# Tap combinations of the first image's convolution on Pool and ACT instead of DVE, and two column combinations per step instead of three

## The chip, the core and the metric

The kernel runs on one core of one Trainium2 chip. The core has a matrix engine (PE, with a separate weight load that the profile calls PEld), three engines for elementwise work (DVE, ACT and Pool, also called GpSimd), and a queue engine (SP) that here only issues DMAs. Each engine works through its own list of instructions in order, and waits on semaphores for the others. The metric is the device time of one execution in microseconds (us).

## The reference, cut to what matters

Eight images of 32 x 32 positions and 256 channels pass through a layer of convolution beside attention with relative positions, then a dense attention layer and a feed-forward layer. Only the first layer matters here:

```
# per image, after a group norm over 32 groups of channels
conv_out = conv3x3(x, conv_w) + conv_b            # 256 -> 192 channels, SAME
k, q, v  = split(x @ qkv_w + qkv_b)               # 64 channels each, 8 heads of 8
logits   = q . k + rel_w(q, key_rel_w) + rel_h(q, key_rel_h)   # 1024 x 1024 a head
attn     = softmax(logits) @ v @ attn_w + attn_b  # 64 channels
x        = x + concat(conv_out, attn)
```

All data and weights are float32.

## The kernel before, in words

**Convolution.** The 3x3 convolution is computed four output columns at a time with combinations of the input columns and of the taps (a Winograd scheme along a row). Along a row, the taps w0, w1 and w2 of `conv_w` become six combinations, and the columns of the normed image become six differences; then six sets of products are made on PE and summed. The tap combinations are made once, by `conv_weights` (lines 298 to 321), into the tile `convw`; each of the six has 128 partitions x 1152 elements. They are

```
cw0 = -(w0 + w1 + w2)/6      cw3 = (w0 - 2 w1 + 4 w2)/24
cw1 = -(w0 - w1 + w2)/6      cw4 = w0/4
cw2 = (w0 + 2 w1 + 4 w2)/24  cw5 = w2
```

Before, DVE makes the six two-input sums (L306, L308, L311, L314, L316, L319), and ACT the two that only scale or copy (L304, L305) and the four scalings in place (L309, L312, L317, L320). The raw taps lie in the tile `taps`.

The column differences are made for every image by `by_fours` (L370 to L411) into the tile `gdif`, on DVE. It reads the normed image x and yields after each small group of operations, so that a caller can spread it over other work. The products are in `conv_steps` (matmuls at L560, tile pc, copied by ACT at L569).

**The norm.** `norm_steps` (L329 to L367) transposes the image on PE, takes statistics on DVE, averages them over groups by two small matmuls (gm, then pv) and forms 1/sqrt in `one_over_root` (L90 to L102): rv = pv + eps on DVE (L96), a logarithm and an exponential on ACT (ry L97, gr L98), then on DVE a correction of four tiny operations (L99 to L102, of which L99 and L100 multiply rv by gr). With gr, DVE writes the normed image x (L360). Pool adds the biases l0b to the image T there (L340).

**Keys, queries and relative logits.** `input_steps` (L418 to L527) makes keys and queries (pk on PE L423; kq by ACT L433 and DVE L440), values (pvv L444), and sends kq by 16 DMAs on SP's queue into the tiles km (L458). The fixed patterns of km come from `key_patterns`: DVE makes a small table oh (L281 to L283), Pool copies and adds it (L289, L290). Then come the relative logits: 256 small matmuls along the width and 256 along the height, in four groups (prel, L495). Each group's two halves are copied out by DVE (L507) and ACT (L509), into rw for the width and into rh for the height. rw is stored to memory (rwd, L512) and also transposed on PE into rwq (tpw L520, copies L522 and L524). The difference table reld for the height is made in turns by DVE and Pool (L262, L265).

**Attention.** A `Unit` is half of one group of heads. Its tile F is gathered by DMAs on SP from rh (L590), kq (L594) and rwd (L601); then follow scores on PE (lg, L618), their maxima on DVE (L626), scores the other way (st, L658), exponentials on ACT (L666) and products with the values (L675). Steps of the convolution are mixed in between.

**Buffers.** The tiles F, x, rw and taps share one pool of three buffers (tag "F"). A new tile of that tag waits for the last reader of the tile whose buffer it takes.

**Order.** For the first image all of this is a prologue (L1024 to L1044), in a block where the order of PE's and DVE's instructions is the one written, and ACT, Pool and SP are ordered by the scheduler. After the norm, the key patterns and the first 12 steps of `input_steps`, a loop runs over the remaining steps, and after each step it takes three steps of `other`, which is the chain of `by_fours` and `conv_weights`. What is left of `other` follows the loop.

Of the kernel before, what the change touches and what calls it, by code (L numbers as in the profile page):

```python
# [3 lines left out]

# [9 lines left out]
ALU = mybir.AluOpType  # L14
# [22 lines left out]
def kernel(  # L37
# [26 lines left out]
    nc = tc.nc  # L64
# [39 lines left out]
    with ExitStack() as ph:  # L104
# [70 lines left out]
        taps = work.tile([P, 4096], FP, tag="F", name="taps", bufs=3)[:, 0 : 9 * KC * CO]  # L175
# [98 lines left out]
        def key_patterns():  # L274

            KM = []
            oh = wp.tile([P, 16 + DH], FP, tag="oh", name="oh")  # L280
            nc.vector.tensor_copy(oh[:, 0:1], esel[:, 0:1])  # L281
            nc.vector.tensor_tensor(oh[:, 1:16], esel[:, 1:16], esel[:, 0:1].to_broadcast([P, 15]), ALU.add)
            nc.vector.tensor_copy(oh[:, 16:24], esel[:, 24:32])  # L283
            for i in range(NG):
                km = wp.tile([P, 2, 4, P], FP, tag=f"km{i}", name=f"km{i}")
                for a in range(2):
                    kv = km[:, a].rearrange("p g (y x) -> p g y x", y=8)
                    for g in range(4):
                        nc.gpsimd.tensor_copy(kv[:, g], oh[:, 0:16].unsqueeze(1).to_broadcast([P, 8, 16]))  # L289
                        nc.gpsimd.tensor_tensor(  # L290
                            kv[:, g], kv[:, g], oh[:, 16:24].unsqueeze(2).to_broadcast([P, 8, 16]), ALU.add
                        )
                KM.append(km)
            return KM
# [3 lines left out]
        def conv_weights(taps):  # L298


            taps = taps.rearrange("p (a b n) -> p b a n", a=3, b=3)
            w0, w1, w2 = (taps[:, i] for i in range(3))
            cw = [convw[:, v] for v in range(NV)]
            nc.scalar.mul(cw[4], w0, 0.25)  # L304
            nc.scalar.copy(cw[5], w2)  # L305
            nc.vector.tensor_tensor(cw[1], w0, w2, ALU.add)  # L306
            yield
            nc.vector.tensor_tensor(cw[0], cw[1], w1, ALU.add)  # L308
            nc.scalar.mul(cw[0], cw[0], -1.0 / 6)  # L309
            yield  # L310
            nc.vector.tensor_tensor(cw[1], cw[1], w1, ALU.subtract)  # L311
            nc.scalar.mul(cw[1], cw[1], -1.0 / 6)  # L312
            yield
            nc.vector.scalar_tensor_tensor(cw[3], w2, 4.0, w0, ALU.mult, ALU.add)  # L314
            yield
            nc.vector.scalar_tensor_tensor(cw[2], w1, 2.0, cw[3], ALU.mult, ALU.add)  # L316
            nc.scalar.mul(cw[2], cw[2], 1.0 / 24)  # L317
            yield
            nc.vector.scalar_tensor_tensor(cw[3], w1, -2.0, cw[3], ALU.mult, ALU.add)  # L319
            nc.scalar.mul(cw[3], cw[3], 1.0 / 24)  # L320
            yield


        def norm_steps(b, held):
# [45 lines left out]
        def by_fours(xn):  # L370


            two = nc.vector.tensor_tensor

            def stt(out, one, factor, two):
                for a in range(2):
                    nc.vector.scalar_tensor_tensor(out[:, a], one[:, a], factor, two[:, a], ALU.mult, ALU.add)

            for part in range(2):
                for kc in range(KC):  # L380
                    d1, d2, d3, d4 = (xn[:, kc, :, :, j].rearrange("p a c x -> p a x c") for j in range(4))
                    v = [gdif[:, i, kc, 1 : HH + 1, :].rearrange("p (a x) c -> p a x c", a=2) for i in range(NV)]
                    if part == 0:

                        stt(v[2], d2, -4.0, d4)
                        yield
                        stt(v[3], d1, -4.0, d3)
                        yield
                        two(v[4], d4, d2, ALU.subtract)
                        two(v[5], d3, d1, ALU.subtract)  # L390
                        yield
                        two(v[0], v[2], v[3], ALU.add)
                        two(v[1], v[2], v[3], ALU.subtract)
                        yield
                        continue

                    stt(v[2], v[5], 2.0, v[4])
                    yield
                    stt(v[3], v[5], -2.0, v[4])
                    yield  # L400


                    stt(v[4], d2, -4.0, v[4])
                    yield
                    stt(v[4][:, :, :, 1:NQ], d4[:, :, :, 0 : NQ - 1], 4.0, v[4][:, :, :, 1:NQ])
                    yield
                    nc.vector.tensor_scalar(v[5], v[5], -4.0, None, ALU.mult)
                    two(v[5], v[5], d3, ALU.subtract)
                    two(v[5][:, :, :, 0 : NQ - 1], v[5][:, :, :, 0 : NQ - 1], d1[:, :, :, 1:NQ], ALU.add)
                    yield  # L410
# [618 lines left out]
        with tc.manual_schedule(engines={mybir.EngineType.PE, mybir.EngineType.DVE}):  # L1029
            held = {}  # L1030
            half_w, half_h, reld_steps = tables()
            for _ in norm_steps(0, held):
                pass
            KM = key_patterns()
            steps = input_steps(0, held)
            for _ in range(4 + NT):
                next(steps)
            reld_steps()
            other = chain(by_fours(held["xn"]), conv_weights(taps))
            for _ in steps:  # L1040
                for _ in range(3):
                    next(other, None)
            for _ in other:
                pass  # L1044
        with tc.manual_schedule(engines={mybir.EngineType.PE, mybir.EngineType.Pool}):
            conv = Conv(0)
            means = []
            for b in range(B):
# [11 lines left out]
                now, held = held, {}  # L1060
# [322 lines left out]
```

## Time and profile before

| what | value |
|---|---|
| median of 3 runs | 2334.63 us (2334.57 to 2335.14) |
| the profiled execution | 2339.52 us, of which its span is 2337.5 us |
| PE busy | 2259.4 us, 97% of the span, mean clock 0.982 |
| DVE busy | 1481.7 us, 63% |
| ACT busy | 955.1 us, 41% |
| Pool busy | 505.3 us, 22% |
| PE busy in the first of 40 slices (58 us each) | 5 tenths |

The profile is of one execution and lists each group of equal instructions as start, duration, engine, line of the code, operation, output and inputs, shapes and count; in brackets stands the idle time of the engine before it and what ended it. In grouped rows the first number after the bar is the busy time and the second the mean duration in ns. PEclk is the clock granted to PE as a share of full speed.

The first 75 us hold all of the prologue. The windows of 5 us in which it ends, with busy time (and count) of PE, PEld, DVE, ACT and Pool, the clock, the share of DMA time and GB/s:

```profile
core 0: us, PE busy (x) PEld busy (x) DVE busy (x) ACT busy (x) POOL busy (x), PEclk, DMA share, GB/s
45.00:50.00 5.00, 4.88 (x128) 4.59 (x124) 4.89 (x14) 0.59 (x1) 0.00 (x0) 0.50 0.37 146
50.00:55.00 5.00, 3.20 (x13) 2.55 (x12) 4.93 (x6) 2.98 (x3) 0.00 (x0) 0.50 0.39 96
55.00:60.00 5.00, 5.00 (x24) 4.61 (x23) 4.88 (x4) 2.35 (x4) 0.00 (x0) 0.80 0.60 112
...
70.00:75.00 5.00, 5.00 (x31) 3.06 (x32) 3.49 (x5) 0.48 (x1) 0.54 (x1) 0.94 0.64 125
```

Between 45 and 60 us DVE is busy nearly throughout, Pool does nothing, and PE works at half of its clock for most of the time.

### The profile page before, as it was taken

The numbers are of one execution on the slowest core, as the hardware profiler recorded it, in microseconds if no ns is written. First come the engines' busy times: TensorE is split into PE (matmuls) and PEld (weight loads), VectorE is DVE, ScalarE is ACT, GpSimd is POOL, SyncE is SP. The second block draws the span as 40 slices with busy tenths as digits, with TensorE's granted clock in tenths as the row PEclk, the third lists the DMA queues.
The fourth block names the chain that finished last, engine by engine and source line by source line (L and its number), as shares of the span: only waits on it lengthen the run. The fifth ranks groups of instructions, "written<-read, shape, count | busy, mean of one in ns | idle before, by whom it ended". The sixth has DMA issues, their size and how long they took to land. (4 is left out here: it accounts for less than half of the span.)

```text
span 2337.5 us, 41910 instructions
## 1 busy us (share of the span) xinstructions
PE 2259.4 (97%) x17273; PEld 1284.4 (55%) x17273; DVE 1481.7 (63%) x2717; ACT 955.1 (41%) x1645; POOL 505.3 (22%) x478
## 2 busy tenths in 40 slices
PE   5999999999999999999999999999998699999998
PEld 5535753664367437733763475357533566666665
DVE  7777587658756775777477748765872624444443
ACT  2255336434643563256325532553364223333332
POOL 3301240213031203300340034012301022222220
PEclk7999999999999999999999999999998799999999
DMA  3520352125122502250333025202420312222200
GB/s 105 103 50 10 58 104 39 41 48 102 22 56 42 109 5 60 56 93 3 60 89 61 7 56 105 45 27 47 82 38 1 108 50 78 78 74 78 72 37 27
DMA packets 71471, 135.85 MB, mean 58 GB/s; under 512 B 12001, under 2 KB 24169, under 8 KB 69233
## 3 DMA queue, kind: packets, MB, share of 16 engines
q1 hardware_dynamic: 65488, 115.47, 23.5%
q0 software_dynamic: 3056, 15.73, 2.0%
q8 instruction: 137, 2.24, 0.4%
q10 hardware_dynamic: 2736, 1.97, 0.3%
q14 instruction: 54, 0.43, 0.1%
HBM read 53.43 MB, written 25.17 MB: 34 GB/s over the span
## 5 line engine op out<-in xcount | busy, mean ns | idle before, releaser
L626 DVE TENSOR_REDUCE my<-lg 128x32 f32<-128x1024 f32 x512 | 617.4, 1222 | 166.3 <-PE st L658 124.9
L666 ACT ACTIVATE PT<-st 128x512 f32<-128x512 f32 (+1 forms) x944 | 542.2, 632 | 313.6 <-PE st L658 309.9
L658 PE MATMUL st<-F,km 32*128 32x512 f32 x2048 | 536.9, 640 | 8.2 <-DMA F<-mb 8.2
L618 PE MATMUL lg<-km,F 24*128 24x512 f32 x2048 | 504.9, 637 | 1.7 <-DMA F<-rh 1.7
L675 PE MATMUL po<-PT,vall 128*32 128x256 f32 (+1 forms) x3200 | 312.5, 452 | 2.4 <-ACT PT L666 2.4
L675 PEld LDWEIGHTS po<-PT,vall 128*32 128x32 f32 x3200 | 66.0, 108 | 312.8 <-issue 279.5
L618 PEld LDWEIGHTS lg<-km,F 24*128 24x128 f32 x2048 | 144.1, 183 | 163.7 <-issue 122.7
L560 PE MATMUL pc<-convw,gdif 128*128 128x192 f32 x1152 | 229.4, 342 | 0.7 <-ACT convw L309 0.7
L1296 PE MATMUL phd<-n2T,w 128*128 128x512 f32 x512 | 223.7, 595 | 0.0
L1313 PE MATMUL py<-w,hT 128*128 128x256 f32 x1024 | 223.6, 379 | 0.0
L658 PEld LDWEIGHTS st<-F,km 32*128 32x128 f32 x2048 | 175.6, 183 | 78.2 <-issue 40.5
L560 PEld LDWEIGHTS pc<-convw,gdif 128*128 128x128 f32 x1152 | 186.9, 192 | 56.4 <-issue 32.0
L1313 PEld LDWEIGHTS py<-w,hT 128*128 128x128 f32 x1024 | 194.6, 190 | 33.3 <-issue 7.7
L340 POOL TENSOR_TENSOR T<-T,l0b 128x2048 f32<-128x2048 f32 x8 | 36.3, 4534 | 617.6 <-PE tpx L333 617.6
L1320 DVE TENSOR_TENSOR r<-py,n 128x256 f32<-128x256 f32 x64 | 27.2, 425 | 213.0 <-PE py L1313 213.0
L1296 PEld LDWEIGHTS phd<-n2T,w 128*128 128x128 f32 x512 | 97.2, 191 | 116.1 <-issue 108.9
L846 POOL TENSOR_TENSOR T<-T,n 128x256 f32<-128x256 f32 x64 | 47.4, 749 | 392.4 <-DVE n L832 392.4
L1303 ACT ACTIVATE hT<-phd,b1c 128x512 f32<-128x512 f32 x128 | 86.3, 686 | 98.3 <-PE phd L1296 98.1
L569 ACT COPY m<-pc 128x384 f32<-128x384 f32 x48 | 23.0, 480 | 242.6 <-PE pc L560 198.1
L901 PE MATMUL lg<-qkv 128*128 128x512 f32 x256 | 121.1, 595 | 0.0
L910 DVE TENSOR_REDUCE nm<-lg 128x1 f32<-128x1024 f32 x64 | 78.1, 1221 | 67.5 <-PE lg L901 67.5
L932 PE MATMUL po<-pt,qkv 128*128 128x256 f32 x512 | 116.5, 380 | 0.0
(250 smaller groups left out, 2584.7 us busy)
## 6 DMA issues: line engine op xcount, KB each, us to landing
F<-rh SPq DMA_DIRECT2D x256, 128.0 KB
F<-kq SPq DMA_DIRECT2D x256, 64.0 KB
F<-rwd SPq DMA_DIRECT2D x256, 64.0 KB
w<-in_L_ffn_W_dram SPq DMA_DIRECT2D x32, 512.0 KB
rwd<-rw SPq DMA_DIRECT2D x16, 512.0 KB
Td<-T POOLq DMA_DIRECT2D x8, 1024.0 KB, 4.2
T<-Td SPq DMA_DIRECT2D x8, 1024.0 KB
out_dram<-yo SPq DMA_DIRECT2D x16, 512.0 KB
```

The source lines that it names most:

```text
L560: nc.tensor.matmul(pc[:, v, :], lhsT=gflat[:, 2 * pair + v, kc, at : at + P], rhs=convw[:, 2 * pair + v, dy, kc * CO : (kc + 1) * CO], sta ...
L618: nc.tensor.matmul(lg[:, a, :], lhsT=self.F[r : r + 24, a, 0, i * P : (i + 1) * P], rhs=KM[self.g][r : r + 24, a].rearrange("p e k -> p (e ...
L626: nc.vector.tensor_reduce(my[:, :, hl], lg.rearrange("p a (y x) -> p y a x", y=WW), AX.XY, ALU.max)
L658: nc.tensor.matmul(st[:, i, :] if len(heads) > 1 else st, lhsT=KM[self.g][r : r + 32, a, e, :], rhs=self.F[r : r + 32, a, e, :], start=Tru ...
L666: nc.scalar.activation(self.pts[j][:, hs, :], st, AF.Exp)
L675: nc.tensor.matmul(self.po[32 * hl : 32 * hl + 32, cols], lhsT=vall[:, j, h * (DH + 1) : h * (DH + 1) + 32], rhs=self.pts[j][:, hl, cols], ...
L901: nc.tensor.matmul(lg[:, h, :], lhsT=qk[0][:, i * P : (i + 1) * P], rhs=qk[1][:, h * 512 : (h + 1) * 512], start=True, stop=True,)
L910: nc.vector.tensor_reduce(nm, lg, AX.X, ALU.max, negate=True)
L932: nc.tensor.matmul(po[:, 0:IB], lhsT=v1[:, jc, :], rhs=pt[:, jc, :], start=jc == 0, stop=jc == NT - 1)
L1296: nc.tensor.matmul(phd, lhsT=ws[k][0][:, kc, f * P : (f + 1) * P], rhs=n2T[:, kc, q * 512 : (q + 1) * 512], start=kc == 0, stop=kc == KC - 1,)
L1303: nc.scalar.activation(hT[:, k * NF + f, :], phd, AF.Gelu, bias=b1c[:, f, k * B + b : k * B + b + 1])
L1313: nc.tensor.matmul(py, lhsT=hT[:, k * NF + f, j * P : (j + 1) * P], rhs=ws[k][1][:, f, :], start=k == 0 and f == 0, stop=k == TOPK - 1 and ...
```

## The change

`conv_weights` is no longer a generator that runs behind `by_fours`. It is called once, before the loop over the steps. Its six sums go to Pool, as plain two-input additions and subtractions; what DVE had fused into them (4 w2 and 2 w1) is made by two more scalings on ACT, in the places of cw3 and cw4, so that cw4 is written with its own value last. The loop takes two steps of `other` after each step, which is now `by_fours` alone. Nothing else differs; the images after the first use the same code as before.

```
+            add = nc.gpsimd.tensor_tensor
+            nc.scalar.copy(cw[5], w2)
+
+            nc.scalar.mul(cw[3], w2, 4.0)
+            nc.scalar.mul(cw[4], w1, 2.0)
+            add(cw[1], w0, w2, ALU.add)
+            add(cw[0], cw[1], w1, ALU.add)
+            nc.scalar.mul(cw[0], cw[0], -1.0 / 6)
+            add(cw[1], cw[1], w1, ALU.subtract)
+            nc.scalar.mul(cw[1], cw[1], -1.0 / 6)
+            add(cw[3], cw[3], w0, ALU.add)
+            add(cw[2], cw[3], cw[4], ALU.add)
+            nc.scalar.mul(cw[2], cw[2], 1.0 / 24)
+            add(cw[3], cw[3], cw[4], ALU.subtract)
+            nc.scalar.mul(cw[3], cw[3], 1.0 / 24)
             nc.scalar.mul(cw[4], w0, 0.25)
-            nc.scalar.copy(cw[5], w2)
-            nc.vector.tensor_tensor(cw[1], w0, w2, ALU.add)
-            yield
-            nc.vector.tensor_tensor(cw[0], cw[1], w1, ALU.add)
-            nc.scalar.mul(cw[0], cw[0], -1.0 / 6)
-            yield
-            nc.vector.tensor_tensor(cw[1], cw[1], w1, ALU.subtract)
-            nc.scalar.mul(cw[1], cw[1], -1.0 / 6)
-            yield
-            nc.vector.scalar_tensor_tensor(cw[3], w2, 4.0, w0, ALU.mult, ALU.add)
-            yield
-            nc.vector.scalar_tensor_tensor(cw[2], w1, 2.0, cw[3], ALU.mult, ALU.add)
-            nc.scalar.mul(cw[2], cw[2], 1.0 / 24)
-            yield
-            nc.vector.scalar_tensor_tensor(cw[3], w1, -2.0, cw[3], ALU.mult, ALU.add)
-            nc.scalar.mul(cw[3], cw[3], 1.0 / 24)
-            yield
...
             reld_steps()
-            other = chain(by_fours(held["xn"]), conv_weights(taps))
+            conv_weights(taps)
+            other = by_fours(held["xn"])
             for _ in steps:
-                for _ in range(3):
+                for _ in range(2):
                     next(other, None)
             for _ in other:
                 pass
```

Pool's and ACT's orders are the scheduler's in both kernels. In the program that is built from the changed kernel, Pool's six sums stand behind its last two reld operations and ahead of the km patterns, in the order cw1 = w0 + w2, cw3 = 4 w2 + w0, cw0, cw2, cw1, cw3. On ACT the order is: the copy to cw5, the scalings to 4 w2 and 2 w1, the scaling of cw0, ry (the logarithm of the norm), the scaling of cw2, gr (its exponential), the scalings of cw1 and cw3, cw4, and then the two kq operations.

## The prediction

> **What bounds the kernel now.** I read the page's busy shares first: TensorE (PE) is busy for 2259.4 of 2337.5 us, 97%. Its clock row then names the weak places, and the first slice is the worst (5 tenths busy). Everything the change touches runs once, in the prologue of the first image, so I left the page and read the timeline of the first 75 us engine by engine. From about 71 us on PE has no gaps, so what counts is one number: how much earlier or later PE reaches that unbroken work. The timelines of ACT, DVE and Pool before the first matmuls of the image show (start, duration, engine, line, tiles):
>
> ```profile
> 19.56 0.20 ACT L97 ACTIVATE ry<-rv 128x2 f32<-128x2 f32 x1 [1.97 <-DVE rv L96]
> 19.79 0.20 ACT L98 ACTIVATE gr<-ry 128x2 f32<-128x2 f32 x1
> ...
> 17.48 0.46 DVE L348 TENSOR_TENSOR dm<-gmv,gm 128x2 f32<-128x2 f32 x1
> 17.98 0.51 DVE L349 TENSOR_TENSOR dm<-dm 128x2 f32<-128x2 f32 x1
> 18.53 0.16 DVE L350 TENSOR_TENSOR dm<-dm,gmv 128x2 f32<-128x2 f32 x1
> ...
> 20.82 0.74 DVE L360 TENSOR_SCALAR x<-xT,gm,gr 128x512 f32<-128x512 f32 x1
> ...
> 17.32 1.15 POOL L265 TENSOR_TENSOR reld<-bdh 128x192 f32<-128x192 f32 x2
> ```
>
> All of the image waits for one thin chain: rv on DVE, Ln and Exp (ry, gr) on ACT, two tiny products and a correction on DVE, then x at 20.82. PE's pk follows at 21.61. ACT is idle for 1.97 us before ry, so today nothing stands in that chain's way.
>
> The other end is the start of attention (SP's and PE's timelines):
>
> ```profile
> 50.17 0.68 SPq L590 DMA_DIRECT2D F<-rh  x1
> ...
> 59.55 1.12 PE L618 MATMUL lg<-km,F 24*128 24x512 f32 x2
> 62.38 3.29 PE L618 MATMUL lg<-km,F 24*128 24x512 f32 x6 [1.72 <-DMA F<-rh]
> 65.61 4.21 PE L560 MATMUL pc<-convw,gdif 128*128 128x192 f32 x12
> 69.74 1.54 PE L618 MATMUL lg<-km,F 24*128 24x512 f32 x8
> 71.22 2.06 PE L560 MATMUL pc<-convw,gdif 128*128 128x192 f32 x11
> ```
>
> The first scores wait 1.72 us for a DMA into F. That series began at 50.17, because F took the buffer of x, which DVE reads until 50.11 (last column combination).
>
> **What leaves DVE.** Six operations of 128x1152, at 50.03 to 58.81, 1.35 or 1.36 us each: 8.1 us. PE's first conv (54.02) waited for the ACT scaling of one of them. With them early, conv matmuls fill the gaps around the tpw transposes.
>
> **What Pool gets.** Six adds of 128x1152. Pool shows no such shape; these groups are near (busy us, mean ns):
>
> ```profile
> L1287 POOL TENSOR_TENSOR T<-T,bet 128x1024 f32<-128x1024 f32 x16 | 40.3, 2516 | 0.0
> L340 POOL TENSOR_TENSOR T<-T,l0b 128x2048 f32<-128x2048 f32 x8 | 36.3, 4534 | 617.6 <-PE tpx L333 617.6
> ```
>
> Scaled by width: 4534 x 1152/2048 = 2.55 us, 2516 x 1152/1024 = 2.83. The second row includes waits behind DVE, so I take 2.6. Pool is free at 18.47, when its two reld operations end. The built order puts the adds there in the order cw1, cw3, cw0, cw2, cw1, cw3, ahead of the km patterns. They end at 21.1, 23.7, 26.3, 28.9, 31.5 and 34.1. The km patterns (23.73 now) need oh, which DVE makes after x, so they move with x and pay nothing of their own. SP's km DMAs need them and kq and move alike.
>
> **What ACT gets, and what is queued behind it.** ACT's order is made by the scheduler: copy and two scalings, then the cw0 scaling (waits for the third add), **ry**, the cw2 scaling (waits for the fourth add), **gr**, then the rest. So the thin chain stands behind two waits. cw0 ends at 26.3 + 1.16 = 27.5 and ry runs; cw2 ends at 28.9 + 1.16 = 30.1; gr runs to 30.3 instead of 19.99. Loss so far: 10.3 us. The two scalings and cw4 that follow end near 36.5, before kq needs ACT: nothing. The delay that the first add gives dm (18.53) is hidden, since ry can't run before 27.5.
>
> **The two products behind gr.** Now DVE forms rv x gr twice, both inputs in SBUF, while Pool is in its fifth and sixth add. The row first: DVE's L348 and L349 took 0.46 and 0.51 us while Pool's two reld ran, and L350, just after them, 0.16. So each such operation loses about 0.3 us to a Pool operation of 0.6. The Trainium skill, "SBUF — State Buffer", section "SBUF: two separate sides", says more: the port pair is an exclusive lock for a whole instruction, and a DVE operation with two SBUF inputs blocks fully against a Pool operation that reads SBUF. By the row as a fixed 0.3 us, x comes 0.6 later still: shift 10.9. By the rule the first product waits for the fifth add's end (31.5), the second for the sixth's (34.1): 34.1 + 0.05 + 0.44 (today's 20.38 to 20.82) puts x at 34.6, a shift of 13.7. In the later images L348 ended right when L340's 4.53 us on Pool ended (1.00 us at 194.46, Pool until 195.44), which speaks for the rule. I take **13.7**; 10.3 is the other end.
>
> **What comes back.** All in a frame shifted by 13.7, so that old times can be compared. DVE now does two column steps between copies of relative logits: rw is copied 1.0 us earlier (37.48 to 36.5: the 1.0 us of L389 and L390) the first time and 2.1 earlier the second (42.20 to 40.1), and the first rh copy ends at 44.15. The first F now takes the buffer of taps, free since the adds, so its DMAs wait only for that rh copy: 44.18 instead of 50.17. **6.0 us** back. The second unit's F now waits for the last column combination instead, but its DMAs stood at 67.4 and aren't needed for another 20 us: nothing. The score waiting at 62.38 starts at 56.4.
>
> The rest hangs on the clock. The windows of 5 us (columns: busy and count of PE, weight loads, DVE, ACT, Pool; clock; DMA share; GB/s):
>
> ```profile
> 60.00:65.00 5.00, 3.28 (x8) 0.95 (x6) 1.23 (x1) 1.20 (x2) 3.08 (x4) 0.88 0.59 126
> 65.00:70.00 5.00, 5.00 (x17) 3.96 (x20) 1.23 (x1) 0.00 (x0) 0.00 (x0) 0.50 0.60 81
> ```
>
> After a window with little PE work the clock was 0.50 for 65 to 70 us, and twelve conv matmuls took 4.21 us there against about 2.2 later. If the new gap doesn't cause that, six scores (paced by maxima of 1.23) take 1.8, twelve conv 2.1 (2.06 x 12/11 x 0.94, the clock of 70 to 75), eight scores 1.54: 56.4 + 5.4 = 61.8, where 71.22 stood. Back: **9.4 us**. If it does, the old durations stay and only 6.0 come back.
>
> The Trainium skill, "TensorE: Matmul & The Clock Gate", section "Part 1: The HAM clock gate", lets the clock fall after an idle window of about 3.4 us. The gap here was 1.72 us and the clock fell all the same, in a window that held mostly scores, which use 24 of 128 rows. By the rule taken literally the clock never falls here and 9.4 come back; by the row a similar stall of 1.7 us can do it again and 6.0 come back. I lean to 9.4, because the conv matmuls that moved forward stand next to the gap and fill its window with full-array work.
>
> **Sum.** +13.7 - 9.4 = **+4.3 us**. Against the profiled execution: 2339.52 to 2343.8. That execution lies 4.9 us above the median of the runs; the difference carries over: 2334.63 + 4.3 = **2338.9 us**, 0.18% slower. About 0.2% (4.7 us) is what a measurement of this kernel can tell from no change, so this sits just inside it.
>
> **Rivals.**
> - *The clock falls again* at the score stall: 13.7 - 6.0 = +7.7, 2342.3. For it: the row above. Against: the conv work beside the gap. It decides as soon as one window of 3.4 us there is mostly scores and waiting.
> - *Pool doesn't block the products* (or its adds are shorter): 10.3 - 9.4 = +0.9, 2335.5; with adds of 2.4 us the fourth ends 0.8 earlier, and the result is even. For it: image 1's rows show only 0.3 us. Against: the later images.
> - *The gain outweighs the wait* (not slower): gr would have to come before the cw2 scaling at run time, which a queue in order excludes; or the stage after 71 us gains from a better clock phase. The regain has to exceed 13.7, so 4.3 us more than I see. With one window of half clock saved later (3.4 us at half speed is 1.7) on top of the unblocked products: 0.9 - 1.7 = -0.8, 2333.8.
> - *F doesn't come earlier*, because its DMAs stay bound by km's DMAs or their own transfers: +13.7, 2348.3. Against: km's end at 39.1, five us before.
>
> **Chances.** Forecast 0.42, clock falls 0.33, unblocked 0.13, F late 0.07, gain 0.05. The forecast's own range is 2336.5 to 2341 (adds of 2.5 to 2.8 move the shift by 0.6 to 1.2, later clock phases by 1.7), a good third of it above the bound. Range 2335.2 to 2343.5: it reaches over the fallen clock and most of the unblocked case. Slower: 0.15 of the forecast, nearly all of the fallen clock and of F late, and the long tail of both: 0.52. Same: 0.44. Faster: 0.04.
>
> **What would show it.** In the profile after: Pool's adds of 2.6 us from 18.5; ry near 27.5, gr near 30; two products of over 1 us each; x near 34.6; F's first DMA near 57.9; the conv that stood at 71.22 near 75.5 with the clock at 1.00 from 70 to 75. If gr stands at 20, or x before 31, the prediction is wrong in its first half; if that conv stands at 79, in its second.

## The result, and the profile after

| | before | changed |
|---|---|---|
| median (range, runs) | 2335.14 us (2334.57 to 2337.86, 5) | 2347.03 us (2345.43 to 2347.64, 5) |
| ratio, 95% interval | | 1.0045 (1.0034 to 1.0056) |
| profiled execution | 2339.52 us | 2345.43 us |
| its span | 2337.5 us | 2343.7 us |

The change made the kernel slower by 0.45%, some 10.5 us of 2335 (the two medians lie 11.9 us apart). The forecast was +4.3 us and 2338.9 us, and its range ended at 2343.5, so the result lies outside it. Note that the two profiled executions differ by only 5.9 us: the one of the kernel before lay 4.9 us above the median that the forecast used, the one of the changed kernel is the fastest of these five. That turns out to be most of the story.

The first half of the prediction stands in the timelines of the changed kernel (start, duration, engine, line, tiles). ACT first, then Pool, then DVE:

```profile
26.36 1.16 ACT L310 ACTIVATE convw<-convw 128x1152 f32<-128x1152 f32 x1 [7.62 <-POOL convw L309]
27.43 0.19 ACT L96 ACTIVATE ry<-rv 128x2 f32<-128x2 f32 x1
28.93 1.16 ACT L315 ACTIVATE convw<-convw 128x1152 f32<-128x1152 f32 x1 [1.32 <-POOL convw L314]
30.00 0.19 ACT L97 ACTIVATE gr<-ry 128x2 f32<-128x2 f32 x1
...
28.86 2.62 POOL L311 TENSOR_TENSOR convw<-convw,taps 128x1152 f32<-128x1152 f32 x1
31.43 2.62 POOL L316 TENSOR_TENSOR convw<-convw 128x1152 f32<-128x1152 f32 x1
...
30.22 1.27 DVE L98 TENSOR_TENSOR rv<-rv,gr 128x2 f32<-128x2 f32 x1 [8.17 <-ACT gr L97]
31.53 2.54 DVE L99 TENSOR_TENSOR rv<-rv,gr 128x2 f32<-128x2 f32 x1
34.10 0.17 DVE L100 TENSOR_SCALAR rv<-rv 128x2 f32<-128x2 f32 x1
34.30 0.16 DVE L101 TENSOR_TENSOR gr<-gr,rv 128x2 f32<-128x2 f32 x1
34.50 2.72 DVE L357 TENSOR_SCALAR x<-xT,gm,gr 128x512 f32<-128x512 f32 x4
```

ry and gr stand behind two scalings that wait for Pool. The two products, 0.16 us of work each, end at 31.49 and 34.07, right where Pool's fifth and sixth add end (31.48 and 34.05). x is at 34.50 instead of 20.82.

The second half, SP's and PE's timelines of the same execution:

```profile
57.98 0.68 SPq L587 DMA_DIRECT2D F<-rh  x1
...
68.84 2.22 PE L615 MATMUL lg<-km,F 24*128 24x512 f32 x6
71.50 1.09 PE L615 MATMUL lg<-km,F 24*128 24x512 f32 x2 [0.43 <-DMA F<-kq]
72.52 3.69 PE L557 MATMUL pc<-convw,gdif 128*128 128x192 f32 x12
76.13 1.30 PE L615 MATMUL lg<-km,F 24*128 24x512 f32 x8
77.36 2.22 PE L557 MATMUL pc<-convw,gdif 128*128 128x192 f32 x12
```

F's first DMA came at 57.98, that is 44.28 in the shifted frame, against 50.17. The block of twelve conv matmuls that stood at 71.22 now stands at 77.36; it is called the second block below. From there on the shift stays near that: 6.14 us here, 6.2 at the end of the span.

### The profile page after: what moved, and what is told of

Same layout as the page of the kernel before. It is cut to its first block, busy times and chain, and to the rows that moved or that the text cites. A ratio compares the mean times of both kernels' runs of the same rounds, so it can differ in the third digit from the quotient of the medians.

```text
span 2343.7 us, 41912 instructions
## 1 busy us (share of the span) xinstructions
PE 2256.7 (96%) x17273; PEld 1283.4 (55%) x17273; DVE 1482.1 (63%) x2711; ACT 957.3 (41%) x1647; POOL 520.6 (22%) x484
## 5 line engine op out<-in xcount | busy, mean ns | idle before, releaser
L1301 ACT ACTIVATE hT<-phd,b1c 128x512 f32<-128x512 f32 x128 | 86.3, 686 | 98.5 <-PE phd L1294 98.3
```

Source lines behind the costliest of these rows:

```text
L1301: nc.scalar.activation(hT[:, k * NF + f, :], phd, AF.Gelu, bias=b1c[:, f, k * B + b : k * B + b + 1])
```

## The experiments

**The kernel before, once more.** Its timed runs lay up to 5 us under its profiled one, so here is another profiled execution of the unchanged kernel.

> The kernel before, once more, to see what differs between its profiled execution (2339.52 us) and its timed runs (2334.6 to 2337.9). Theory (clock beside the first scores): in an execution near 2335 us the clock does not fall to half at about 64 us, the twelve conv matmuls that took 4.21 us at 65.61 take about 2.2, and the conv that stood at 71.22 us stands near 67.5. Rival (the 4.9 us lie elsewhere, in the half-clock stretches at 1753 to 1873 us): the first 80 us look as in the first profile and the late stretches are shorter.

The profiled execution took 2334.93 us. 13 runs lay between 2334.93 and 2340.29, median 2336.94. PE's timeline at the same place:

```profile
60.62 1.12 PE L618 MATMUL lg<-km,F 24*128 24x512 f32 x2
62.21 2.45 PE L618 MATMUL lg<-km,F 24*128 24x512 f32 x6 [0.47 <-DMA F<-rh]
64.59 2.22 PE L560 MATMUL pc<-convw,gdif 128*128 128x192 f32 x12
66.73 1.14 PE L618 MATMUL lg<-km,F 24*128 24x512 f32 x8
67.81 2.22 PE L560 MATMUL pc<-convw,gdif 128*128 128x192 f32 x12
```

Its windows there (columns as before; the clock stands behind Pool's count):

```profile
60.00:65.00 5.00, 4.50 (x15) 1.92 (x14) 1.53 (x2) 1.54 (x2) 3.08 (x4) 1.00 0.59 124
65.00:70.00 5.00, 5.00 (x36) 3.79 (x34) 2.98 (x3) 0.00 (x0) 0.00 (x0) 1.00 0.60 81
```

The score waits until nearly the same time (62.21 against 62.38), but the clock is 1.00 from 60 on. The twelve conv matmuls take 2.22 us instead of 4.21, and the second block stands at 67.81 instead of 71.22. Same program, 3.4 us apart at that block, and 4.5 us at the end of the span (2333.0 against 2337.5). The theory held; of the other 1.1 us, about 1.0 lie later, where this execution lacks a stretch of half clock that the first had at 1753 us (and the changed kernel at 1759).

**ACT's queue freed.** The five operations of ACT that wait for Pool go behind kq.

```
-            nc.scalar.mul(cw[0], cw[0], -1.0 / 6)
+            with tc.issue_after(kqops[0]):
+                nc.scalar.mul(cw[0], cw[0], -1.0 / 6)
...
```

> The changed kernel with ACT's five convw operations that wait for Pool queued behind both kq operations, so that ry and gr wait for nothing of the tap combinations. Theory (ACT's queue holds most of the loss): gr near 22.5 us instead of 30.0 (dm still waits for Pool's first add), x near 26.7 instead of 34.5, and the time falls by 4 to 8 us against the changed kernel; less than 7.8 if DVE's eight reld subtractions now wait for Pool's km patterns, which still end near 44. Rival (the shift of x is not what costs): time within 2 us of the changed kernel though x stands 8 us earlier.

Median 2345.25 us (2344.13 to 2346.40), 1.8 less than the changed kernel, with ranges that overlap, and not the 4 to 8 that I expected. DVE's timeline of this kernel:

```profile
22.06 1.23 DVE L98 TENSOR_TENSOR rv<-rv,gr 128x2 f32<-128x2 f32 x1 [0.51 <-ACT gr L97]
23.32 2.53 DVE L99 TENSOR_TENSOR rv<-rv,gr 128x2 f32<-128x2 f32 x1
25.88 2.54 DVE L100 TENSOR_SCALAR rv<-rv 128x2 f32<-128x2 f32 x1
28.45 2.52 DVE L101 TENSOR_TENSOR gr<-gr,rv 128x2 f32<-128x2 f32 x1
31.02 4.96 DVE L364 TENSOR_SCALAR x<-xT,gm,gr 128x512 f32<-128x512 f32 x4
```

gr came at 21.82, 8.2 us earlier, but then four tiny operations waited for one add of Pool each (the second to the fifth end at 23.26, 25.83, 28.40 and 30.96), and the first part of x for the last one. Matmul pk began at 34.06 instead of 35.30. So my theory gave ACT's queue too much: the adds block the chain on DVE on their own, and the wait on ACT only lies on top of the same time. I had counted two waiting operations because in the changed kernel the other three come after Pool's last add.

**Products with one input each.**

```
-        nc.vector.tensor_tensor(v, v, out, ALU.mult)
-        nc.vector.tensor_tensor(v, v, out, ALU.mult)
+        for _ in range(2):
+            for i in range(v.shape[-1]):
+                nc.vector.tensor_scalar(v[:, i : i + 1], v[:, i : i + 1], out[:, i : i + 1], None, ALU.mult)
```

The function also serves the dense layer's norm, where this form corrects only the first of eight groups of tokens; that part of the computation is changed.

> The changed kernel with the two products rv x gr as four operations of one column each, whose second factor comes as a scalar operand. Theory (the products wait for Pool's adds because both inputs come through SBUF ports): the products end near 31.0 us instead of 34.1, x near 31.4 instead of 34.5, time 2 to 4 us less than the changed kernel. Rival (a scalar operand waits as well, or the wait has another cause): x stays near 34.5 and the time is unchanged.

Four products took 0.58 us together from 30.15, while Pool's fifth add ran to 31.39, so they did not wait. The next two operations did, 0.66 and 2.53 us, to the ends of the same two adds; x came at 34.02, 0.5 earlier. The median was 2348.57 us (2346.74 to 2349.21), no gain where 2 to 4 us were expected. The wait was not removed but passed on to the next operations.

**Taps held longer.** Everything as in the changed kernel, but ACT's 0.25 w0, the last reader of taps, stands behind the second rh copy.

```
+            yield
+            with tc.issue_after(copied[3]):
+                nc.scalar.mul(cw[4], w0, 0.25)
-            nc.scalar.mul(cw[4], w0, 0.25)
```

> The changed kernel with the last read of taps (ACT's 0.25 w0 into cw4) moved behind the second rh copy of ACT, so that F's buffer comes free near 65.3 us instead of 36.3. Theory (the earlier F DMAs are worth what they moved): F's first DMA near 65.3 instead of 57.98, the scores 7 us later, time 5 to 8 us more than the changed kernel. Rival (F's DMAs are hidden anyway): time unchanged within 1 us.

F's first DMA came at 65.07, and the median was 2353.32 us (2352.67 to 2355.41), 6.3 more than the changed kernel, for 7.1 us that F's first DMA came later. The buffer that F takes is worth nearly what it moves, although the clock has a part in it: in the profiled execution it was at half from 72.6 to 86.3, in the changed kernel's only from 73.1 to 76.5.

**Without the adds.** The same as ACT's queue freed, with Pool's six adds taken out. The combinations, and with them the convolution of the first layer, are not computed; the matmuls all stay.

```
-            add(cw[1], w0, w2, ALU.add)
-            add(cw[0], cw[1], w1, ALU.add)
-            nc.scalar.mul(cw[0], cw[0], -1.0 / 6)
+            with tc.issue_after(kqops[0]):
+                nc.scalar.mul(cw[0], w0, -1.0 / 6)
...
```

> The changed kernel without Pool's six adds: ACT's scalings read the raw taps, so the combinations of the taps and with them the first layer's convolution are left out; ACT's last five scalings stand behind kq. All else is the changed kernel. Theory (Pool's adds beside the norm hold the whole loss): x near 20.9 us as before, F's first DMA near 44.2 instead of 57.98, time 15 to 18 us less than the changed kernel and 5 to 8 less than the kernel before. Rival (part of the loss comes from the other edits, such as two steps instead of three): x near 20.9, but the time not below the kernel before.

x came at 20.73, F's first DMA at 44.23, the median was 2332.32 us (2330.17 to 2334.67): 14.7 less than the changed kernel, and 0.9983 (0.9976 to 0.9991) of the kernel before, 4.2 us by the medians measured side by side. Both fall short of what I expected. Against ACT's queue freed it is 12.9 us less, and the two differ only in the adds and in what ACT's scalings read. This splits the change: Pool's adds, with ACT's wait for them, cost some 14.7, the rest brings 4. PE's timeline shows why only 4:

```profile
53.63 1.12 PE L615 MATMUL lg<-km,F 24*128 24x512 f32 x2
57.74 2.94 PE L615 MATMUL lg<-km,F 24*128 24x512 f32 x6 [2.99 <-DMA F<-kq]
60.61 3.64 PE L557 MATMUL pc<-convw,gdif 128*128 128x192 f32 x12
64.18 1.14 PE L615 MATMUL lg<-km,F 24*128 24x512 f32 x8
65.25 2.22 PE L557 MATMUL pc<-convw,gdif 128*128 128x192 f32 x12
```

The waiting score comes at 57.74, not 6.0 but 4.5 us before the 62.21 of the kernel before: from the first DMA into F to this score it took 13.5 us instead of 12.1. PE waits 2.99 us for it, and the twelve conv matmuls behind it take 3.64: the clock was at half from 56.7 to 63.5. The second block is ahead by 2.6 us.

**Two steps alone.**

```
-                for _ in range(3):
+                for _ in range(2):
```

> The kernel before with two steps of the combinations after each step instead of three, nothing else. Theory: the copies of rw and rh come 1 to 3 us earlier, but F still waits for the last column combination near 50 us, so the time stays within 1.5 us of the kernel before. Rival (the earlier copies alone bring the gain): F's first DMA near 44 us and 4 to 6 us less.

F's first DMA came at 51.83, and the ratio is 0.9995 (0.9986 to 1.0003): no difference, as expected.

**x in another buffer.** Two steps, tap combinations on DVE as before, and F free from the start.

```
-            xn = f_tile("x").rearrange("p a e s -> p (a e s)")[:, 0 : KC * S]
+            xn = pt_tile("x") if b == 0 else f_tile("x").rearrange("p a e s -> p (a e s)")[:, 0 : KC * S]
```

> The kernel before with two steps, and with the first image's x in a buffer of another tag, so that F has a free buffer from the start. Tap combinations stay on DVE behind the column combinations. Theory: F's first DMA near 44.2 us instead of 50.1, but the maxima can't start before DVE ends the tap combinations and the rwq copy near 60, so of the 6 us only 2 to 4 come back. Rival (F's DMAs are all that counts): 6 us less than the kernel before. Other rival: nothing, because convw sets the start of the convolution.

F's first DMA came at 44.58, the ratio is 0.9988 (0.9981 to 0.9995), 2.1 us less by the medians. DVE ended the tap combinations at 60.7 and PE's first conv stood at 56.45 behind the first of them, so the theory fits: the buffer alone brings a part of it.

**Tap combinations in DVE's gaps.** Four of the six operations go where DVE waits for kq. The km pattern is one block repeated sixteen times, so it is made once and spread by ACT, which keeps Pool still.

```
+            weights = conv_weights(taps)
+            for i in range(4 + NT):
+                if i in (1, 3 + NT // 2):
+                    next(weights)
+                    next(weights)
+                next(steps)
...
+            other = chain(weights, by_fours(held["xn"]))
```

> The kernel before with the tap combinations on DVE, but four of the six in DVE's two waits for kq (23.7 to 26.3 and 27.1 to 30.2 us) and two right after reld; two steps. To keep Pool away from them, the km pattern is made once on DVE before the norm (it is the same block sixteen times) and spread by three ACT copies before the taps land. Theory: x near 20.9, F's first DMA near 44.5 (taps' buffer), the convolution's first matmul near 46, and 5 to 7 us less than the kernel before, so near 2329 to 2331. Rival (the first stage is bound by something else, such as the DMAs of F or the clock): within 2 us of the kernel before.

Median 2333.97 us (2330.85 to 2337.33), ratio 0.9985 (0.9977 to 0.9993): 2.5 us less than the kernel before, half of what I expected. The profiled execution was its slowest: F's first DMA came at 47.39, after pk had run slow (the second four matmuls took 3.16 us, against 1.94 in the kernel before), and the clock was at half from 58.6 to 68.8.

**The convolution held back.** In all kernels with early tap combinations PE takes conv matmuls ahead, between the transposes. Two kernels undo that alone: the changed one, and the one with the gaps.

```
+                            if b == 0 and not first:
+                                first.append(1)
+                                hold = tc.issue_after(turned[0].ins)
```

> The changed kernel with the first image's convolution held behind the last tpw transpose on PE, as in the kernel before; nothing else. Theory (moving conv matmuls ahead takes away what kept the clock up at the first scores): with 24 conv rows in one block right before the scores there is no half clock in the 10 us after them, the second block of twelve conv rows after the first scores starts at 75 to 76.5 us instead of 77.36, time 1 to 3 us less than the changed kernel. Rival (work done early is time gained): PE has 5 us more to do after the transposes, that block starts near 80, time 2 to 4 us more.

> The version with the tap combinations in DVE's gaps, with the convolution held behind the last tpw transpose in the same way. Theory: no half clock after the first scores, 1 to 3 us less than without the hold (2333.97), so 2331 to 2333, 3 to 5 us less than the kernel before. Rival: 2 us or more above 2334.

> The changed kernel once more, beside the two versions with the hold. Theory (the clock falls at the first scores because little full-array work is left there): a stretch of half clock of one or two windows between 69 and 80 us again, time 2345 to 2348. Rival (chance of the phase): none this time, and the time near 2343.5.

The changed kernel again: 2346.87 us (2345.04 to 2348.06), ratio 1.0045 (1.0031 to 1.0059), with the half clock at the first scores from 70.3 to 77.1. Held, it took 2345.22 (2343.39 to 2348.11): 1.65 less, but the ranges overlap, and its profiled execution, its slowest, has half clock from 72.4 to 79.2, with 24 conv matmuls right before the scores. So the hold does not keep the clock up every time. In that execution the second block stood at 80.00, as the rival said. With the gaps, the hold gave 2332.41 us (2329.64 to 2335.85), 0.9983 (0.9977 to 0.9990) of the kernel before: 3.9 us less by the medians. Here too the clock was at half after the first scores, from 60.3 to 63.7, which the theory had excluded, and 0.9983 is not told apart from the 0.9985 without the hold: what the hold is worth is not shown. This is still the fastest version that computes the whole result. DVE's timeline of it:

```profile
23.43 1.35 DVE L310 TENSOR_TENSOR convw<-taps 128x1152 f32<-128x1152 f32 x1
24.82 1.36 DVE L312 TENSOR_TENSOR convw<-convw,taps 128x1152 f32<-128x1152 f32 x1
26.29 0.74 DVE L446 TENSOR_SCALAR kq<-pk,kqb 64x512 f32<-64x512 f32 x1
26.95 1.34 DVE L315 TENSOR_TENSOR convw<-convw,taps 128x1152 f32<-128x1152 f32 x1
28.22 1.34 DVE L318 SCALAR_TENSOR_TENSOR convw<-taps 128x1152 f32<-128x1152 f32 x1
30.15 0.74 DVE L446 TENSOR_SCALAR kq<-pk,kqb 64x512 f32<-64x512 f32 x1 [0.58 <-ACT kq L439]
...
31.74 2.23 DVE L265 TENSOR_TENSOR reld<-bdh 128x192 f32<-128x192 f32 x8
```

The four operations fit between kq's, which stay at 26.29 and 30.15 (26.31 and 30.21 before), and reld, which took 3.64 us beside Pool's km patterns, takes 2.23.

## Why the prediction was wrong

- **Shift of x, +13.7.** Right: 34.50 minus 20.82 is 13.68, with the adds at 2.61 to 2.63 us each. Its division was not: 10.3 for ACT's queue and 3.4 for the products. With the queue freed pk gained 1.2 us; without the adds the shift is gone. The adds are the cause. ACT's queue and DVE's own waits lie over the same time, so taking one away leaves most of the shift to the other.
- **The rule on the port pair.** The wait for whole instructions was right, and a fixed 0.3 us would have been wrong. It reached further than I used it: the correction with a single SBUF input (L100 of the freed kernel, 2.54 us) waited too.
- **F's DMAs, -6.0.** Right, in their start (57.98, forecast 57.9) and in what reached the scores. The same matmuls have to be compared. Counted within the first group of eight, the third began at 62.38 before and the seventh at 63.70; in the changed kernel they began at 69.74 and 71.50 (before, then changed):

```profile
63.70 1.97 PE L618 MATMUL lg<-km,F 24*128 24x512 f32 x2
...
69.74 1.32 PE L615 MATMUL lg<-km,F 24*128 24x512 f32 x4
71.50 1.09 PE L615 MATMUL lg<-km,F 24*128 24x512 f32 x2 [0.43 <-DMA F<-kq]
```

  Less the shift, the third came 6.3 us earlier (56.0, forecast 56.4) and the seventh 5.9.
- **The step that failed: "Back: 9.4 us".** Of it 6.0 are F's and came back. The other 3.4 are for a clock that no longer falls at the first scores, and it fell there in both profiled executions of the changed kernel, at 73.1 and at 70.3. The conv that was to stand near 75.5, or at 79 with such a fall, stood at 77.36. From the seventh score to the second block it took 7.5 us in the first profiled execution of the kernel before and 5.9 in the changed kernel, so 1.7 of the 3.4 came back. Against the second one (4.2 us, no fall) nothing came back, and 1.6 were lost; in the changed kernel's second execution (7.0 us) 2.8.
- **"The difference carries over."** This sentence cost more than the sum. The median was missed by 8.1 us. Only 1.6 of them are in the sum, which forecast 2343.8 for the profiled execution and got 2345.43. The other 6.5 come from moving the sum to the median: the first profiled execution lay 4.9 us above its median, the changed kernel's 1.6 below. The fall of the clock, worth 3.4 us at the second block, was the greater part of what set that first execution apart. The sum took it as a gain, and a baseline without it was then used: the same gain was counted twice. How many timed runs of the kernel before had the fall is not known; of 113 on record 22 took 2339 us or more, as that execution did.
- **"Conv matmuls stand next to the gap and fill its window."** Wrong. In all thirteen profiled executions, each recorded stretch at one clock, but for the one that the end of the program cuts off, is a whole multiple of 3.41 us. In the changed kernel the last such 3.41 us before the fall (first row: all of PE; second: conv alone) held little conv, though PE waited only 0.43 us in it. The second execution of the kernel before had as much PE work in 59.17 to 62.58, more of it conv, and no fall:

```profile
69.67:73.09 3.42, 2.98 (x10) 1.39 (x10) 1.69 (x2) 0.00 (x0) 2.91 (x4) 1.00 0.56 87
69.67:73.09 3.42, 0.57 (x3) 0.57 (x4) 0.00 (x0) 1.00 0.56 87
...
59.17:62.58 3.41, 2.94 (x13) 1.92 (x14) 0.74 (x1) 1.54 (x2) 1.22 (x3) 1.00 0.66 135
59.17:62.58 3.41, 1.52 (x9) 1.22 (x8) 0.48 (x1) 1.00 0.66 135
```

  It is so in all thirteen. In the ten with a fall at the first scores, the 3.41 us before it held at most 0.90 us of conv and transposes; in the three without one, the first group of scores and the block behind it lay in stretches that each held at least 1.41. Where these stretches lie differs from execution to execution of one program (by 1.2 us between the two of the kernel before), and with it whether scores and waiting fill one of them. This is a pattern read from traces, and no run moved it at will.

The sum, mended: at the second block the change cost 9.55 us against the second profile of the kernel before (77.36 - 67.81). The shift is 13.6 of it, 5.7 came back with F's scores (the seventh stood at 63.57 there), and 1.6 is clock. Over the whole span it is 10.7 (2343.7 - 2333.0), beside the 10.5 of the ratio. The rival "clock falls again" had the right reason, one window of 3.4 us that is mostly scores and waiting, and still the wrong time, since it used the same baseline.

What stays open: what sets the place of the 3.41 us stretches in an execution, and how much work of which kind in one of them keeps the clock up.

## What to carry to other kernels

An add on Pool is not free time because Pool is idle: look at what DVE does beside it. Tiny operations in a chain, each waiting for one large Pool instruction, cost the sum of the Pool instructions; put such work where DVE itself waits for PE or ACT, even on DVE. When a single profiled execution lies above the timed runs, find out where before summing against it: a gain that removes what only that execution had is no gain.

## What the runs showed of the hardware

- A DVE operation can wait for a run of Pool instructions, not only for one. In the changed kernel the first of eight reld subtractions took 2.23 us (the others 0.35) from 45.02 to 47.25; Pool's chain of km patterns, each 0.30 to 0.42 us, ended at 47.04:

```profile
45.02 2.23 DVE L264 TENSOR_TENSOR reld<-bdh 128x192 f32<-128x192 f32 x1
...
46.26 0.78 POOL L289 TENSOR_TENSOR km<-km,oh 128x128 f32<-128x128 f32 x2
```

- A TENSOR_SCALAR of 128x2 with one SBUF tensor waited like the ones with two (2.54 us), while products of 128x1 with a scalar operand did not (0.58 us for four).
- The clock fell at the first scores after a 3.41 us stretch in which PE was busy for 2.98 us, 0.57 of them conv, and did not fall after one with 2.94 us, 1.52 of them conv. Busy time alone did not keep it up; the scores use 24 of 128 rows.
- The same program takes 2334.2 to 2340.7 us from execution to execution, a width of 6.5 us, more than most of the parts measured here. At one place a fall of the clock made 3.4 of them.
